# Two graph-attention layers on one core: two more nested Strassen products per matrix, added up inside one PSUM bank, and the order of every engine taken from a list schedule in the source

## The chip, the cores and the metric

The kernel runs on one core of one Trainium2 chip. The metric is the device time of one execution in microseconds (us); lower is better. A core has five instruction queues that matter here: PE (TensorE, the matrix array; its weight loads are shown apart as PEld), DVE (VectorE), ACT (ScalarE), POOL (GpSimd) and SP (SyncE, which here only issues DMAs). Each engine works through its own queue strictly in order. All arithmetic is in 32-bit floats.

## The reference

There are 128 independent graphs of 128 nodes with 512 features, and two attention layers of 8 heads, the second on the output of the first:

```python
# layer 0
Q, K, V = (x @ W + b for W, b in ...)            # 8 heads of 64
scores  = Q K^T / 8 + a_i + c_j + b_g + log(adj + 1e-9)    # a = x @ w_g[:D], c = x @ w_g[D:]
x       = softmax(scores) @ V + x
# layer 1
q, k, v = (x @ W.T + b for W, b in ...)
logits  = q k^T / 8 + log(max(adj, 1e-8))
out     = (softmax(logits) @ v) @ Wo.T + bo
x       = layer_norm(x + out) * gamma + beta
```

## The kernel before, in words

**Tiling.** Four graphs are one group, so that a projection is a 512 x 512 by 512 x 512 product. `t` counts 64 steps: `t` below `NG` = 32 is layer 0 of group `t`, the rest is layer 1 of group `t - NG`. A step has the matrices v, q and k, and in layer 1 the output projection o of the group before it. That makes 223 matrices in all; the o of the very last group is done graph by graph with plain matmuls. The exponentials of the scores are multiplied by the adjacency (`weigh`), which takes the place of adding its logarithm. Layer 0 writes its result to DRAM (`x1d`), and layer 1 reads it again.

**Strassen twice.** Every matrix is computed by Winograd's form of Strassen's scheme: seven products P1 to P7 of 256 x 256 blocks instead of eight (`Strassen`). The sums of weight blocks are made once (`combine_outer`), the sums T1 to T4 of input blocks once for each step, by POOL (`sums`). A plain product (`product`, L280) is 8 matmul instructions that stream 256 columns; one instruction fills one half of the output partitions, and the two halves run side by side in the array. Inside some of the seven products the same scheme is used again (`inner`, L339): seven products of 128 x 128 blocks, that is 14 matmul instructions that stream 128 columns. In the text these are **wide** and **narrow** matmuls. `INSIDE` (L174) says where: in P2 and P4 of nearly all matrices, in P2 alone or nowhere at the start of each layer. The inner products run in four phases. After each phase DVE adds pieces of the PSUM bank onto a copy in SBUF (`onto`, `add`), and the outer additions are done in the same instructions.

**Biases and rows.** The q and k biases are added by ACT while it copies from PSUM (`copy`). The v bias of layer 0 and the o bias of layer 1 are added to the natural-layout input tile `xn` by POOL (`add_row`, L267); `onto_x` and `residual` (L548), both on POOL, then add `xn` to the result.

**Attention.** `scores` (L444) takes all four graphs of a group in one go: 32 matmuls that use half the array's rows each (64 x 128 tiles, shown as 64\*128), where every projection matmul uses half of its columns (128 x 64 tiles, shown as 128\*64). Two double-sized PSUM buffers, and two banks borrowed from the projections for the third graph, hold them. ACT takes the exponential, DVE multiplies by the adjacency, `mix` forms attention times v for two graphs at a time, and DVE normalises.

**Order.** Each instruction is kept where the program has it (`InOrder`, every instruction is recorded on L132, so that all lines of the profile say L132 and the tiles' names tell them apart). The order is written by hand: a row of slots, seven to a matrix (`SLOTS`, L55), says which product comes when, and `put(pre/post, slot, ...)` hangs every load, sum, addition and store on a slot. Tiles come from pools with two to four buffers; the sums T1 to T4 have two each.

Of the kernel before, what the change touches and what calls it, by code (L numbers as in the profile page):

```python
# [41 lines left out]
class Strassen:  # L42

    A11, A12, S4, NA22, S1, S2, S3 = range(7)

    SLOTS = (("P1", "P4.1 b"), ("P4 b",), ("P3 b", "P4.2 b"), ("P6", "P4.3 b"), ("P5", "P4.4 b"), ("P7",), ())  # L55
# [5 lines left out]
    PHASES = {"1": ("P1", "P2", "P5"), "2": ("P6",), "3": ("P7",), "4": ("P4", "P3")}  # L61


    RAW = {(0, 0): A11, (1, 0): A12, (1, 1): NA22, (0, 1): S3}

# [25 lines left out]
    @staticmethod  # L91
    def combine_inner(v, t, x, ks=slice(0, 2)):

        q, x = t[:, Strassen.A12 : Strassen.NA22 + 1 : 2][:, ks], x[:, ks]
        low, high = slice(0, P), slice(P, 2 * P)
        Strassen.combine(
            v, q[:, :, 0, low], q[:, :, 1, low], q[:, :, 0, high], q[:, :, 1, high], x[:, :, 0], x[:, :, 1], x[:, :, 2]
        )

    @staticmethod  # L100
    def inner_weight(t, x, i):

        k = i == "P4"
        q, low, high = t[:, Strassen.NA22 if k else Strassen.A12], slice(0, P), slice(P, 2 * P)
        return {
            "P1": q[:, 0, low], "P2": q[:, 1, low], "P3": x[:, k, 2], "P4": q[:, 1, high],
            "P5": x[:, k, 0], "P6": x[:, k, 1], "P7": q[:, 0, high],
        }


class InOrder:


    ENGINES = ("tensor", "vector", "scalar", "gpsimd", "sync")

    def __init__(self, tc):
        self.nc = tc.nc
        for name in self.ENGINES:
            setattr(self, name, InOrder.Engine(tc, getattr(tc.nc, name)))

    def __getattr__(self, name):
        return getattr(self.nc, name)

    class Engine:
        def __init__(self, tc, engine):
            self.tc, self.engine = tc, engine

        def __getattr__(self, name):
            f = getattr(self.engine, name)
            if not callable(f):  # L130
                return f
            return lambda *args, **kw: self.tc.keep_in_program_order(f(*args, **kw))  # L132


def fast_path(ctx, tc, args, GOOD, bad):
# [5 lines left out]

# [3 lines left out]
    nc = InOrder(tc)  # L149
# [6 lines left out]
    SCALE = 1.0 / HD**0.5  # L156
    HALVES = slice(0, P // 2), slice(P // 2, P)
    assert N == P and HD == 64 and KC == 4 and G == 4 and NG * G == B

    const = ctx.enter_context(tc.tile_pool(name="const", bufs=1))  # L160
    weights = ctx.enter_context(tc.tile_pool(name="weights", bufs=4))
    act = ctx.enter_context(tc.tile_pool(name="act", bufs=1))
    work = ctx.enter_context(tc.tile_pool(name="work", bufs=2))
    small = ctx.enter_context(tc.tile_pool(name="small", bufs=2))
# [3 lines left out]
    XTB = [act.tile([P, G, KC, N], F32, name=f"xT_{i}") for i in range(2)]  # L168
    X1D = [dram.tile([G, N, D], F32, name=f"x1d_{g}") for g in range(NG)]
    LAST = 2 * NG  # L170
    XN, XT, TS, AD, QT, KT, V, C, GATE, RC, OR, AT, TO, HS, MV, RS = ({} for _ in range(16))
    WQ, WK, WV, WO, BQ, BK, ROWS = ({} for _ in range(7))

    INSIDE = {t: ("P2", "P4") if t and t != NG else ("P2",) if t else () for t in range(LAST)}  # L174
    INSIDE.update({("qk", NG): (), ("o", NG): ()})
    INSIDE.update({("o", t): ("P2", "P4") if t > NG else () for t in range(NG, LAST)})

# [3 lines left out]

    def load_tiles(t):
        XT[t] = XTB[t % 2]
        AD[t] = act.tile([P, G, N], F32, tag="adjT", name=f"adjT_{t}", bufs=2)

    def load_graph(t, b, engine):

        L, g = split(t)
        src = x[g * G : (g + 1) * G] if L == 0 else X1D[g]
        xs = src.rearrange("b (t i) (c q f) -> q i b c t f", i=S, q=Q, f=S)  # L190
        for q in range(Q):
            rows = slice(q * S, (q + 1) * S)
            engine.dma_start(XT[t][rows, b].rearrange("i c (t f) -> i c t f", f=S), xs[q, :, b])

    def load_adjacency(t, engine):
        _, g = split(t)
        adjs = adj[g * G : (g + 1) * G].rearrange("b (t i) (q f) -> q i (b t) f", i=S, f=S)
        for q in range(Q):
            rows = slice(q * S, (q + 1) * S)
            engine.dma_start(AD[t][rows].rearrange("i b (t f) -> i (b t) f", f=S), adjs[q])  # L200

    def load(t):
        load_tiles(t)
        for b in range(G):
            load_graph(t, b, nc.sync)

    def load_natural(t, *engines):
        L, g = split(t)
        src = x[g * G : (g + 1) * G] if L == 0 else X1D[g]
        for k in range(2):  # L210
            XN[t, k] = act.tile([P, 2, D], F32, tag="xn", name=f"xn_{t}_{k}", bufs=4)
# [22 lines left out]
    def sums(Bs, name, s):  # L234
        a, b = Strassen.SUMS[s]
        Bs[s] = act.tile([P, 2, 2, N], F32, tag=s, name=f"{s}_{name}", bufs=2)
        nc.gpsimd.tensor_tensor(Bs[s], Bs[a], Bs[b], ALU.subtract)

    def inner_sums(Bs, name, i="P2"):

        q = Bs[Strassen.OPERANDS[i][1]]
        y = act.tile([P, 4 if i == "P2" else 3, N], F32, tag=f"inner{i}", name=f"inner{i}_{name}", bufs=2)
        b11, b12, b21, b22 = q[:, 0, 0], q[:, 1, 0], q[:, 0, 1], q[:, 1, 1]
        t1, t2, t4 = (y[:, i] for i in range(3))
        t3 = y[:, 3] if i == "P2" else b12
        nc.gpsimd.tensor_tensor(t1, b12, b11, ALU.subtract)
        nc.gpsimd.tensor_tensor(t2, b22, t1, ALU.subtract)
        nc.gpsimd.tensor_tensor(t3, b22, b12, ALU.subtract)
        nc.gpsimd.tensor_tensor(t4, t2, b21, ALU.subtract)
        Bs[i, "inner"] = {"P1": b11, "P2": b21, "P3": b22, "P4": t4, "P5": t1, "P6": t2, "P7": t3}  # L250


    def gate(t, b, s):

        if (b, s) == (0, 0):
            C[t] = small.tile([P, 2, G], F32, tag="c", name=f"c_{t}", bufs=2)
        nc.gpsimd.tensor_tensor(GW[:, 2 + s], XN[t, b // 2][:, b % 2], GW[:, s], ALU.mult)

    def gate_sum(t, b, s):
        o = GW[:, 2 + s]  # L260
        nc.scalar.activation(o, o, AF.Identity, accum_out=C[t][:, s, b : b + 1])

    def gate_exp(t):
        GATE[t] = small.tile([P, G], F32, tag="gate", name=f"gate_{t}", bufs=2)
        nc.scalar.activation(GATE[t], C[t][:, 0], AF.Exp, bias=bg)

    def add_row(t, k):  # L267


        for b in (1, 0):  # L270
            xn = XN[t, k][:, b]
            nc.gpsimd.tensor_tensor(xn, xn, ROWS[split(t)[0]], ALU.add)


# [5 lines left out]
    def product(i, W, Bs, bank, side, first):  # L280
# [5 lines left out]
        for o in range(2):  # L286
            for k in range(2):
# [5 lines left out]
                matmul(dst, lhsT, rhs, first and o == 0 and k == 0, k == 1)  # L293
# [5 lines left out]
    def matrix(n, name, W, Bs, side, out_tile, dst, bias=None, inside=("P2",)):  # L299

        t = {}
        C12, C21 = block(0, 1, side), block(1, 0, side)

        def bank(tag):
            return ps.tile([P, 4 * N], F32, tag=tag, name=f"{tag}{name}")

        def biased(m):
            return [(slice(2 * k * N, 2 * (k + 1) * N), bias()[:, 2 * m + k : 2 * m + k + 1]) for k in range(2)]  # L310

        def copy(o, i, m):

            if bias is None or m is None:
                if len(o.shape) == 3:
                    i = i.rearrange("p (h d) -> p h d", d=o.shape[2])
                nc.scalar.copy(o, i)
            else:
                for h, b in biased(m):
                    nc.scalar.activation(o[:, h], i[:, h], AF.Identity, bias=b)  # L320

        def kept(tag, i, m, bufs):
            t[tag] = work.tile([P, 4 * N], F32, tag=tag, name=f"{tag}{name}", bufs=bufs)
            copy(t[tag], i, m)

        def add(m, n, i, v, lo=0, hi=4, shift=0):


            for lo, hi, o in dst(m, n, lo, hi):
                p, s = i[:, (lo + shift) * N : (hi + shift) * N], v[:, lo * N : hi * N]  # L330
                if len(o.shape) == 3:
                    p, s = (r.rearrange("p (h d) -> p h d", d=o.shape[2]) for r in (p, s))
                nc.vector.tensor_tensor(o, p, s, ALU.add)

        def onto(v, b, i, at):
            v = v[:, b * N : (b + 1) * N]
            nc.vector.tensor_tensor(v, i[:, at * N : (at + 1) * N], v, ALU.add)

        def inner(i, phase):  # L339

            m, v = (1, t["u3"]) if i == "P4" else (0, t["t1"])
            if phase == "1":
                t[i] = bank("p1") if i == "P2" else t["a"]
            p, a, b = t[i], Strassen.inner_weight(*t["W"], i), t["B"][i, "inner"]
            for k, j in enumerate(Strassen.PHASES[phase]):
                at = {"P2": 0, "P5": C12, "P3": C12}.get(j, C21)
# [740 lines left out]
```

## Time and profile before

| what | us |
|---|---|
| three runs | 3147.54, 3147.86, 3148.11; median 3147.86 |
| profiled execution, first to last instruction | 3146.3 |
| PE busy | 3130.7 |
| POOL busy | 2344.3 |
| DVE busy | 2104.3 |
| ACT busy | 985.2 |

The profiled execution lies 1.6 us under the median of the runs. One step of layer 0 takes 42.7 us and one of layer 1 54.6 us, by the starts of neighbouring score groups in the timeline (1033.58 and 1076.31; 2500.03 and 2554.58). The span is practically one row of matmuls: the first product starts at 8.06 us, the last matmul ends at 3133.9 us, and 12.4 us of layer norm and stores follow. The DMA queue of SP issues 2,578 transfers, about 0.65 us apart when they follow one another.

### The profile page before, as it was taken

To read this page: it belongs to the slowest core of one execution; us is meant where nothing else is said; L and a number is where in the kernel's file an instruction comes from. 1 tells how busy PE (TensorE), PEld (TensorE's weight loads), DVE (VectorE), ACT (ScalarE), POOL (GpSimd) and SP (SyncE) were. 2 spreads that over 40 slices of the span, in tenths; PEclk is the share of its full clock that TensorE was granted. 3 is DMA by queue.
4 is the path that set the end of the run, shared out by engine and by line. 5 is a ranking of instruction groups with operands and counts; after the bars stand their busy time and mean duration, and the time that the engine had idled before them with its cause. 6 is when DMAs were issued, how large, how long until landed. Compare 5 with 4: busy or idle time off the path is not lost.

```text
span 3146.3 us, 102048 instructions
## 1 busy us (share of the span) xinstructions
PE 3130.7 (100%) x42570; PEld 2510.6 (80%) x42570; DVE 2104.3 (67%) x4941; ACT 985.2 (31%) x1927; POOL 2344.3 (75%) x2732
## 2 busy tenths in 40 slices
PE   9999999999999999999999999999999999999998
PEld 7777777777777777777888888788888888787885
DVE  6666666666666666666676667667666766667666
ACT  3333333333333333332222222222222222222222
POOL 8776767676766676786877878787877878787876
PEclk9999999999999999999999999999999999999999
DMA  5333333333333333442434334343434334343432
GB/s 136 81 82 86 85 83 80 74 82 85 86 82 85 69 88 81 101 112 54 100 70 89 82 74 93 76 97 73 96 75 82 89 74 94 75 99 72 95 68 80
DMA packets 1017279, 266.28 MB, mean 85 GB/s; under 512 B 942704, under 2 KB 949872, under 8 KB 1016816
## 3 DMA queue, kind: packets, MB, share of 16 engines
q1 hardware_dynamic: 1015152, 257.34, 37.2%
q8 instruction: 340, 5.57, 0.7%
q10 hardware_dynamic: 1408, 2.10, 0.2%
q14 instruction: 123, 1.01, 0.1%
q0 software_dynamic: 256, 0.26, 0.0%
HBM read 159.92 MB, written 67.11 MB: 72 GB/s over the span
## 4 chain that ended last, share of the span: by engine, by line
PE 99%; DVE 0%; DMA 0%; ACT 0%; issue 0%; ACTq 0%; DVEq 0%
PE p3v L132 10%; PE p0q L132 10%; PE p3k L132 10%; PE av L132 8%; PE p2k L132 7%; PE p2v L132 7%; PE p2q L132 7%; PE p0o L132 7%; PE s L132 6%; PE p0v L132 4%; PE p3q L132 4%; PE p0k L132 4%; PE p2o L132 3%; PE p1k L132 3%; PE p1q L132 3%; PE p1v L132 3%
## 5 line engine op out<-in xcount | busy, mean ns | idle before, releaser
L132 POOL TENSOR_TENSOR gw<-xn,gw 128x512 f32<-128x512 f32 x256 | 323.7, 1281 | 103.6 <-ACT gw L132 100.8
L132 POOL TENSOR_TENSOR xn<-xn,row 128x512 f32<-128x512 f32 x256 | 328.0, 1304 | 2.0 <-DMA bq<-in_L_gnn_bq_dram 2.0
L132 POOL TENSOR_TENSOR T<-xT 128x512 f32<-128x512 f32 x128 | 193.6, 1512 | 138.4 <-DVE xT L132 133.7
L132 POOL TENSOR_TENSOR xn<-o,xn 128x512 f32<-128x512 f32 x128 | 161.0, 1281 | 147.1 <-DVE o L132 147.1
L132 POOL TENSOR_TENSOR h<-h,xn 128x512 f32<-128x512 f32 x124 | 161.2, 1322 | 115.8 <-DVE h L132 115.7
L132 PE MATMUL p3k<-T,wk 128*64 128x256 f32 (+1 forms) x2068 | 234.3, 350 | 0.0
L132 PE MATMUL p3v<-wv,T 128*64 128x256 f32 (+1 forms) x2068 | 225.9, 351 | 0.0
L132 PE MATMUL p0q<-T,wq 128*64 128x256 f32 (+1 forms) x2068 | 225.0, 350 | 0.0
L132 PE MATMUL s<-qT,kT 64*128 64x128 f32 x3088 | 200.4, 276 | 0.2 <-DVE xT L132 0.2
L132 PE MATMUL av<-v,e 128*64 128x65 f32 x6272 | 199.6, 221 | 0.0
L132 PEld LDWEIGHTS av<-v,e 128*64 128x64 f32 x6272 | 196.5, 137 | 0.1
L132 DVE TENSOR_TENSOR e<-e,adjT 128x1024 f32<-128x1024 f32 x98 | 150.7, 1538 | 65.5 <-ACT e L132 65.5
L132 PEld LDWEIGHTS s<-qT,kT 64*128 64x128 f32 x3088 | 182.7, 188 | 11.7 <-issue 11.4
L132 PEld LDWEIGHTS p3k<-T,wk 128*64 128x64 f32 x2068 | 154.1, 137 | 46.5
L132 PEld LDWEIGHTS p3v<-wv,T 128*64 128x64 f32 x2068 | 141.4, 137 | 56.4
L132 PEld LDWEIGHTS p0q<-T,wq 128*64 128x64 f32 x2068 | 142.0, 137 | 54.3
L132 POOL TENSOR_TENSOR h<-h,gamma 128x512 f32<-128x512 f32 x121 | 154.7, 1278 | 27.9 <-ACT h L132 27.9
L132 DVE STREAM_TRANSPOSE xT<-xT 128x512 f32<-128x512 f32 x252 | 173.4, 697 | 0.5 <-DMA xT<-in_x_dram 0.5
L132 ACT ACTIVATE gw<-gw 128x512 f32<-128x512 f32 x256 | 160.9, 630 | 39.1 <-POOL gw L132 39.1
L132 POOL TENSOR_TENSOR h<-h,beta 128x512 f32<-128x512 f32 x121 | 154.9, 1280 | 9.5
L132 PE MATMUL p0o<-wo,T_o 128*64 128x256 f32 (+1 forms) x1368 | 155.6, 353 | 0.5 <-ACT u3o L132 0.5
L132 PEld LDWEIGHTS p0o<-wo,T_o 128*64 128x64 f32 x1368 | 106.7, 137 | 30.1 <-ACT u3o L132 0.8
(315 smaller groups left out, 8088.6 us busy)
## 6 DMA issues: line engine op xcount, KB each, us to landing
x1d<-xn SPq DMA_DIRECT2D x64, 512.0 KB, 3.0
xT<-x1d SPq DMA_DIRECT2D x512, 64.0 KB, 2.5
xn<-x1d SPq DMA_DIRECT2D x64, 512.0 KB, 6.3
xT<-in_x_dram SPq DMA_DIRECT2D x496, 64.0 KB, 2.8
xn<-in_x_dram SPq DMA_DIRECT2D x62, 512.0 KB, 4.5
aT<-o SPq DMA_DIRECT2D x984, 32.0 KB, 1.9
out_dram<-h SPq DMA_DIRECT2D x60, 512.0 KB, 4.5
adjT<-in_adj_dram SPq DMA_DIRECT2D x256, 64.0 KB, 3.7
```

Of the source, the lines that this page charges most:

```text
L132: return lambda *args, **kw: self.tc.keep_in_program_order(f(*args, **kw))
```

## The change

The whole of the fast path is written anew; what is computed stays the same.

1. **Two more nested products.** P1 and P5 also use the inner scheme, in every matrix but six (v, q and k of the first step of each layer, which have none). The program then has 12,152 narrow and 5,544 wide matmul instructions, where it had 6,062 and 9,024.
2. **The inner product is added up within its bank.** ACT first writes zeros into two blocks of the bank. Narrow matmuls accumulate onto what lies there, and between phases ACT copies one block to another and one to SBUF (`s5`), and DVE adds twice within the bank. The outer additions follow on whole banks.
3. **Other work moves.** The v and o biases are added by DVE as it copies from PSUM (`row=ROW`), so that `add_row` is gone. The residual of layer 1 is an accumulating DMA issued from POOL in place of a POOL addition. `root` and `shift` use DVE in part.
4. **Attention one graph at a time.** `scores` has one PSUM buffer of two banks, `mix` one bank and works by half graphs, each at a place of its own. The buffers of the projections are the banks A0, A1, B, C and D. Tiles are placed once; T1 to T4 have a single buffer each.
5. **The order.** `Plan` records every operation with the tiles it touches and a cost from a formula, and `schedule` runs a list scheduler forwards and backwards twelve times over the whole program. Instructions are issued in order of the best start times. A vector operation that waits for a DMA therefore stands in DVE's queue where the formula has the data landed.

In the program order that results, all 256 score groups of 8 matmuls stand alone; before there are 63 of 32 and two of 16.

```diff
-    SLOTS = (("P1", "P4.1 b"), ("P4 b",), ("P3 b", "P4.2 b"), ("P6", "P4.3 b"), ("P5", "P4.4 b"), ("P7",), ())
-    PHASES = {"1": ("P1", "P2", "P5"), "2": ("P6",), "3": ("P7",), "4": ("P4", "P3")}
+    INSIDE = ("P1", "P2", "P4", "P5")
...
+class Plan:
+    HOP, DRAIN, MARGIN = 0.1, 0.17, 0.25
+    PATIENCE, PASSES = 40.0, 12
...
+    def cost(engine, method, aps, accumulates):
...
+        if method == "dma_start":
...
+            return 0.6, 2.2 + kb / 150
+        if engine == "scalar":
+            return (0.15 + 0.00086 * n + 0.2 * accumulates,)
+        if engine == "vector":
+            if method in ("transpose", "bn_stats"):
+                return (0.01 + 0.00133 * n,)
+            return (0.15 + (0.00106 if psum or len(aps) < 3 else 0.00135) * n,)
+        return (0.2 + 0.00215 * n,)
...
+    def wait(self, p, o):
+        if p.engine == o.engine and not p.lag:
+            return 0.0
+        return p.lag + self.HOP + self.DRAIN * (p.engine == "tensor") + self.MARGIN * (o.engine == "tensor")
...
-        def inner(i, phase):
-            m, v = (1, t["u3"]) if i == "P4" else (0, t["t1"])
...
-                matmul(p[:, at * N : (at + 1) * N], x, y, phase == "1" and k == 0, True)
-            if phase == "1":
-                onto(v, 0, p, C21)
-                add(m, 0, p, v, 0, 1)
...
+    def inner(i, W, Bs, bank, side, pos):
...
+        nc.scalar.copy(blocks[:, C21 : 4 : 3 - C21], ZERO)
+        leaves(pos[0], ("P5", 3), ("P1", C21))
+        nc.scalar.copy(s5, blocks[:, 3])
+        nc.scalar.copy(blocks[:, 0], blocks[:, C21])
+        leaves(pos[1], ("P2", 0), ("P6", C21))
+        nc.vector.tensor_tensor(blocks[:, C12], blocks[:, C21], s5, ALU.add)
+        leaves(pos[2], ("P3", C12), ("P7", C21))
+        nc.vector.tensor_tensor(blocks[:, 3], blocks[:, C21], s5, ALU.add)
+        leaves(pos[3], ("P4", C21))
...
+        make("P1", a, True)
+        copy(t1, a, 0)
+        make("P6", a, False)
+        copy(u2, a, 0)
+        make("P2", c, True)
+        add(0, 0, c, t1)
+        make("P7", a, False)
+        copy(u3, a, 1)
+        make("P5", b, True)
+        add(1, 1, b, u3)
+        make("P3", b, False)
+        add(0, 1, b, u2)
+        make("P4", d, True)
+        add(1, 0, d, u3)
...
-    def scores(t, graphs, spare=None):
...
+    def scores(t, b, e, pos):
+        k, s = b // 2, SCORES
+        with nc.unit(pos, 0.92):
+            for c in range(KC):
+                for r in range(2):
...
+                    nc.tensor.matmul(s[:, r, c], KT[k][at], QT[k][at], start=True, stop=True)
+        s = s.rearrange("p r c j -> p (r c) j")
+        nc.scalar.activation(s, s, AF.Exp, scale=SCALE, **({"bias": C[t][:, 1, b : b + 1]} if t < NG else {}))
+        nc.vector.tensor_tensor(e, s, AD[t][:, b : b + 1].to_broadcast([P, H, N]), ALU.mult)
...
-    def residual(t, n):
-        for b in range(2):
-            h = HS[t, n][:, b]
-            nc.gpsimd.tensor_tensor(h, h, XN[t, n][:, b], ALU.add)
+    def residual(t, k):
+        nc.gpsimd.dma_start(HSB[k], X1D[split(t)[1]][2 * k : 2 * k + 2].rearrange("b p d -> p b d"), accum_op=ALU.add)
...
-    for i in range(-1, max(max(pre), max(post), 7 * len(mats) + 3) + 1):
-        for u in pre.get(i, []):
-            u()
...
+    nc.issue()
```

## The prediction, made before the changed kernel had run

> **What bounds the kernel now.** I read the page first, then PE's waits, then the timeline of a stretch of layer 0. TensorE is busy for the whole span at full granted clock:
>
> ```profile
> span 3146.3 us, 102048 instructions
> PE 3130.7 (100%) x42570; PEld 2510.6 (80%) x42570; DVE 2104.3 (67%) x4941; ACT 985.2 (31%) x1927; POOL 2344.3 (75%) x2732
> PEclk9999999999999999999999999999999999999999
> ```
>
> In the table of PE's waits six waits add up to 3.1 us, so nobody holds it up:
>
> ```profile
> engine line waited for: us in total, times, longest us
> PE p0v L132 <- DVE wv L132: 0.9, 1, 0.9
> PE p0o L132 <- ACT u3o L132: 0.5, 1, 0.5
> ```
>
> So the time is the sum of the matmuls' own pace, and the pace is read from starts in the timeline (durations include the pipeline's latency; one matmul shows as two records):
>
> ```profile
> 1020.28 1.90 PE L132 MATMUL p2k<-T,wk 128*64 128x256 f32 x16
> 1022.01 0.39 PE L132 MATMUL p0q<-innerP,wq 128*64 128x128 f32 x4
> 1022.23 0.39 PE L132 MATMUL p0q<-T,wq0i 128*64 128x128 f32 x4
> 1022.44 0.39 PE L132 MATMUL p1k<-innerP,wk0i 128*64 128x128 f32 x4
> 1022.66 1.90 PE L132 MATMUL p3k<-T,wk 128*64 128x256 f32 x16
> 1024.39 0.39 PE L132 MATMUL p1k<-innerP,wk 128*64 128x128 f32 x4
> ```
>
> A plain product takes 1.73 us (1020.28 to 1022.01); three block products take 0.65 us (1022.01 to 1022.66), 0.217 us each, with no gap between different banks or sizes.
>
> **The change, part by part.**
>
> *Matmuls removed.* A nested product is 7 x 0.217 = 1.52 us in place of 1.73, 0.21 us less. Narrow matmuls go from 6,062 to 12,152; at 14 to a product that is 435 products more, so 435 x 0.205 (between 1.73 and 1.72, as other products start) = **-89 us**.
>
> On narrow matmuls a rule speaks against the change: the Trainium skill's page "TensorEngine Tiling (Array Packing)", section Performance Considerations, Instruction Overhead, charges each matmul some 60 cycles, and there are 2,610 more of them; at the 2.4 GHz of "TensorE: Matmul & The Clock Gate" my estimate from the pages would be 65 us lost. The rows above show none: eight wide matmuls take 1.73 us and sixteen narrow ones would take 8 x 0.217 = 1.74.
>
> *Scores alone.* The same timeline shows what a group of scores costs beside its own work, since it uses another shape of tile:
>
> ```profile
> 1033.26 0.39 PE L132 MATMUL p3k<-T,wk0i 128*64 128x128 f32 x4
> 1033.58 2.06 PE L132 MATMUL s<-qT,kT 64*128 64x128 f32 x32
> 1035.47 1.06 PE L132 MATMUL s_p<-qT,kT 64*128 64x128 f32 x16
> 1036.36 1.06 PE L132 MATMUL s<-qT,kT 64*128 64x128 f32 x16
> 1037.35 1.95 PE L132 MATMUL p0v<-wv,T 128*64 128x256 f32 x16
> 1039.13 0.61 PE L132 MATMUL p1v<-wv,xT 128*64 128x128 f32 x8
> ```
>
> The last narrow matmuls would be through at 1033.26 + 0.22 = 1033.48, and the scores begin 0.10 later. One graph in the middle takes 0.89 (1035.47 to 1036.36); the four take 3.77, which is 0.21 more than 4 x 0.89. The product behind them takes 1.78, 0.05 more. So each change to the other shape and back costs 0.36 us, which I take as 0.35 for rounding. The new order has 256 such changes where there were 65: 191 x 0.35 = **+67 us**. The planner's cost of a score group, 0.92, holds only the 0.89. Half graphs of `mix` have the projections' own tile shape and cost nothing: in the timeline a narrow product starts at 1005.85 and `mix` behind it at 1006.07, 0.22 later.
>
> The tensor queue alone thus gives 3147.9 - 89 + 67 = 3126. This is made on the profiled 3146.3 and carried to the median, 1.6 above.
>
> *ACT, DVE, POOL.* Their instructions in the new program by rows of the old:
>
> ```profile
> L132 DVE TENSOR_TENSOR u3k<-p3k,u3k 128x128 f32<-128x128 f32 x141 | 41.1, 292 | 107.6 <-PE p3k L132 104.7
> L132 DVE TENSOR_TENSOR v<-p2v,u3v 128x512 f32<-128x512 f32 x64 | 43.6, 681 | 0.0
> L132 ACT COPY u3v<-p3v 128x512 f32<-128x512 f32 x47 | 27.6, 587 | 203.1 <-PE p3v L132 203.0
> L132 ACT ACTIVATE t1q<-p0q,bq 128x256 f32<-128x256 f32 x94 | 39.5, 471 | 51.7 <-PE p0q L132 51.7
> ```
>
> DVE gets 1,736 block additions (x 0.29 = 503) and 1,081 additions or row copies of 512 columns (x 0.68 = 735); with 252 multiplications by the adjacency at 1.21, 440 transposes at 0.69 and the small operations of normalising I come to some 2,430 us, 78% of the span. ACT gets 868 zero fills and 1,736 block copies, some 770 us by the line through 0.587 at 512 columns and 1.027 at 1,024, and comes to 1,780. POOL loses 256 row additions (328 us in its table) and 124 residual additions (161) and comes to some 2,100. No row shows ACT or DVE adding into a bank; the nearest, ACT's exponential in place in PSUM, costs what the one into SBUF does (1,027 against 1,025 ns), so I take no surcharge; a tenth more would be some 80 us on queues with over 600 us to spare. None becomes the bound as a sum. The cost is in **waits**, since PE depends on round trips PE-DVE-PE and PE-ACT-PE within each nested product, and PE's covers are short:
>
> (a) Round trips by themselves. I laid the new order's matmuls end to end at the paces above and compared every pause of a PSUM tile with the work between at row durations plus 0.26 us for two hand-overs (ACT and DVE start some 0.21 after the last matmul is issued). In 32 of 4,055 pauses the work is longer, by 12 us together: **+12**. This assumes that DVE and ACT are free; at 78% DVE often isn't, but the planner leaves 0.25 on each wait of PE. Low end 0. High end: 0.1 us for each of 868 nested products, 87.
>
> (b) Transfers that DVE waits for. The source lets a 64 KB load land 0.6 + 2.63 = 3.2 us after its issue and puts the transpose there or behind. Rows say:
>
> ```profile
> xT<-in_x_dram SPq DMA_DIRECT2D x496, 64.0 KB, 2.8
> adjT<-in_adj_dram SPq DMA_DIRECT2D x256, 64.0 KB, 3.7
> xn<-x1d SPq DMA_DIRECT2D x64, 512.0 KB, 6.3
> ```
>
> x fits. The adjacency is 0.5 us late at the median, and up to 7.6 - 3.2 = 4.4. While DVE waits for it, the block additions behind it in its queue wait, and PE behind those. 64 steps x 0.5 = 32, less what PE has in hand and what DVE still has to do: in the new order 14 DVE operations, some 5.3 us by rows, stand between the last use of the old adjacency and the transpose of the new. I take **+20**. Low 0, if DVE is busy elsewhere when it lands; high 64 x 1.5 = 96 (SP issues twenty loads in a row 0.05 us slower each than the source has it, 1 us).
>
> (c) The residual's accumulating DMA, 31 times two. No row shows one. Bounds: 3.0 (the 512 KB store to `x1d`) and 12.6 (the 512 KB load at 6.3, paid twice, for it also reads what it adds to). The source allows 0.6 + 5.6; between the two last writes and the first statistics DVE has only 2.4 to 6.6 us of other work. Nearest row: the load, 6.3, on an emptier queue. I take **0**; the high end is (12.6 - 6.4) x 31 = 190. "DMA: Bandwidth & Descriptors", Anatomy of one DMA, fits 2.0 us plus bytes at 436 GB/s for a DMA from POOL; 3.2 us here, an estimate from the page by which it would never be late.
>
> (d) Single buffers for T1 to T4: from the last matmul on the old T4 to the first on the new one lie some 4.1 us of matmuls; POOL needs 1.28 + 0.73. Start and tail: a few us either way. **0**.
>
> Sum: 3126 + 12 + 20 = **3158 us**, 0.3% slower: the saved matmuls are given back by the change of tile shape, and short waits, which were absent before, decide the sign. A measurement of this kernel can tell 0.2%, 6 us, from no change.
>
> **The rivals.**
>
> *Faster: the waits stay hidden* (31%). The score groups make PE 4 x 0.35 = 1.4 us a step slower than planned, and this is slack for everybody else; then (b) is 0 and the time is 3126 + 12 = 3138. For it: the planned margins, and idle DVE time. Against it: a queue in order at 78% in which one late load stops four nested products.
>
> *Much faster: the change of shape is free where it meets a wait anyway* (6%): 3147.9 - 89 + 12 = 3071. Against it: all 65 old changes cost the same, groups of two graphs and of four.
>
> *Slower still: the accumulating DMA holds DVE* (11%). Place: the first statistics of each layer-1 step; price 31 us for each us after 6.4; with a landing at 8.4 it is 62 us, 3220.
>
> *Slower still: DVE's queue makes PE wait in every product* (12%): 868 x 0.1 = 87 in place of the 12, 3233. For it: DVE at 78%; against it: 0.25 us margins.
>
> **How the numbers follow.** The forecast has 40%, with 3140 to 3190 as its own range. Faster by over 0.2% (below 3142): the 6, 24 of the 31 and 4 of the 40, 34%. Within: 7 and 9, 16%. Slower: 27 of the 40 and the two last rivals, 50%. The range 3116 to 3230 leaves out the 6% below and about half of the two slow rivals.
>
> **What would show it.** Nested products at 0.217 a block and narrow records doubled, with wide ones down to three fifths (the first term). Scores standing alone, with 0.1 before them and 0.25 within and behind (second). PE's table of waits: DVE and ACT, with tens of us in total, and in the waits of DVE adjacency and `h` transfers (third). I am wrong if PE's waits stay under 15 us, if the score changes cost less than 0.2, or if PE idles over 100 us.

## The result, and the profile after

The changed kernel takes **3389.6 us** (median of four runs, 3384.41 to 3391.71), the kernel before 3148.0: 1.0765 times as long, 95% interval 1.075 to 1.0781. Its profiled execution spans 3387.9 us, against 3146.3. The page of the changed kernel, with busy time, granted TensorE clock and the shares of the chain of waits:

```profile
span 3387.9 us, 115982 instructions
...
PE 3191.8 (94%) x47790; PEld 2657.8 (78%) x47790; DVE 2240.5 (66%) x5287; ACT 1612.3 (48%) x4396; POOL 2063.8 (61%) x2245
...
PEclk9999999999999999999999999999999999999999
...
PE 68%; SPq 14%; DMA 6%; issue 4%; POOL 4%; DVE 3%; ACT 0%; DVEq 0%; POOLq 0%; ACTq 0%
```

DVE, ACT and POOL are all further from full than forecast. PE is idle for 196 us, where the prediction had named 100 as a sign of being wrong, and the chain runs for 14% of the span through SP's queue, which computes nothing.

**Where the time went, by steps.** From the starts of neighbouring score groups in the timeline (mean of 27 steps in the middle of each layer):

| kernel | layer-0 step | layer-1 step | total |
|---|---|---|---|
| before | 42.7 | 54.6 | 3148.0 |
| changed | 42.7 | 62.2 | 3389.6 |

Layer 0 lost nothing. By the same starts, 4.2 us are lost before the first scores of layer 1 (at 1420.7 instead of 1416.5; the first step alone takes 47.6), 22.6 in the first three steps of layer 1 (178.6 for 156.0), 208.7 in its other 28 (1737.9 for 1529.2) and 6.1 behind the start of the last step's scores: 241.6 us, the whole difference.

**Layer 0 is the tensor queue that was forecast.** PE's timeline there (start, duration, two records to a matmul):

```profile
310.90 0.39 PE L298 MATMUL bankB<-wi,innerT 128*64 128x128 f32 x4
311.12 0.39 PE L298 MATMUL bankB<-w,T 128*64 128x128 f32 x4
311.44 1.16 PE L298 MATMUL s<-qT,kT 64*128 64x128 f32 x16
312.53 0.44 PE L298 MATMUL bankC<-wi,innerB 128*64 128x128 f32 x4
312.80 0.39 PE L298 MATMUL bankC<-w,xT 128*64 128x128 f32 x4
```

A block takes 0.22 (310.90 to 311.12). The scores start 0.10 after the last block is through (311.12 + 0.22), the next block 0.20 after 0.89 of scores, and that block takes 0.05 more: 0.35 us for a visit of the other tile shape.

**In layer 1 DVE waits for transfers.** The largest of PE's waits is now for DVE's additions within bank B, 95.2 us; before, all of PE's together were 3.1. From the table of DVE's waits (for what, us in total, times, longest):

```profile
DVE gw L298 <- DMA gw<-o: 138.3, 37, 5.6
...
DVE xT L298 <- DMA xT<-x1d: 72.4, 60, 3.1
...
DVE adjT L298 <- DMA adjT<-in_adj_dram: 36.3, 22, 3.1
...
DVE st L298 <- DMA h<-x1d: 24.9, 20, 2.6
```

PE waits for DVE, and DVE waits for the moved attention output (`gw`), 37 times in 31 steps and up to 5.6 us, then for `x`, and for the adjacency less than for either; `st`, the statistics of the layer norm, wait for the accumulating DMA. All of DVE's waits for transfers come to 291 us. One such place, first in SP's queue, then DVE's, then PE's (the bracket is the idle time before and what ended it):

```profile
2430.98 10.98 SPq L298 DMA_DIRECT2D gw<-o  x16
2442.06 1.92 SPq L298 DMA_DIRECT2D xT<-x1d  x3
2444.08 11.34 SPq L298 DMA_DIRECT2D gw<-o  x16
```
```profile
2458.02 1.31 DVE L298 STREAM_TRANSPOSE gw<-gw 128x512 f32<-128x512 f32 x2 [4.76 <-DMA gw<-o]
2459.25 0.27 DVE L298 TENSOR_TENSOR bankB<-bankB,s 128x128 f32<-128x128 f32 x1
```
```profile
2455.93 0.39 PE L298 MATMUL bankD<-innerT,wi 128*64 128x128 f32 x4
2459.57 0.44 PE L298 MATMUL bankB<-T,wi 128*64 128x128 f32 x4 [3.26 <-DVE bankB L298]
```

SP issues 35 transfers from 2430.98 to 2455.42, that is 24.4 us, 0.70 us each. The schedule charges 0.6, or 21.0 us, and puts the transposes where the data would have landed by that. They are 3.4 us late before the landing is even counted; DVE stands for 4.76 us, three additions into banks behind the transposes stand with it, and PE has work for part of that time and then stops for 3.26 us. A landing itself is nearly on time at the median: for 32 KB the formula allows 0.6 + 2.4 = 3.0 us, for 512 KB 6.2. Of the 992 moves 233 take longer than their 3.0, up to 8.0; what late landings cost is the question of run 2.

```profile
gw<-o SPq DMA_DIRECT2D x992, 32.0 KB, 2.0
h<-x1d POOLq DMA_DIRECT2D x62, 512.0 KB, 6.4
```

### The profile page after: what moved, and what is told of

The parts are those of the page before. It is cut to its first block, busy times and chain, and to the rows that moved or that the text cites. A ratio compares the mean times of both kernels' runs of the same rounds, so it can differ in the third digit from the quotient of the medians.

```text
span 3387.9 us, 115982 instructions
## 1 busy us (share of the span) xinstructions
PE 3191.8 (94%) x47790; PEld 2657.8 (78%) x47790; DVE 2240.5 (66%) x5287; ACT 1612.3 (48%) x4396; POOL 2063.8 (61%) x2245
## 4 chain that ended last, share of the span: by engine, by line
PE 68%; SPq 14%; DMA 6%; issue 4%; POOL 4%; DVE 3%; ACT 0%; DVEq 0%; POOLq 0%; ACTq 0%
PE bankA L298 24%; PE bankB L298 16%; SPq L298 14%; PE bankC L298 8%; PE bankD L298 7%; PE s L298 7%; PE av L298 6%; DMA h<-x1d 2%; DMA gw<-o 2%; DMA adjT<-in_adj_dram 1%; POOL T L298 1%; DMA xT<-x1d 1%; POOL xn L298 1%; POOL innerB L298 1%; DVE gw L298 1%
## 5 line engine op out<-in xcount | busy, mean ns | idle before, releaser
L298 PE MATMUL bankA<-T,w 128*64 128x256 f32 x4096 | 521.0, 381 | 3.7 <-ACT t L298 3.7
L298 PEld LDWEIGHTS bankA<-T,w 128*64 128x64 f32 x4096 | 274.7, 137 | 93.9 <-ACT t L298 4.9
L298 PE MATMUL bankA<-w,T 128*64 128x256 f32 x2048 | 265.2, 382 | 2.6 <-DVE u L298 2.6
L298 PE MATMUL bankB<-xT,w 128*64 128x256 f32 x2048 | 254.5, 382 | 8.2 <-DVE qT L298 5.1
L298 DVE TENSOR_TENSOR bankB<-bankB,s 128x128 f32<-128x128 f32 x434 | 127.3, 293 | 166.9 <-PE bankB L298 140.8
L298 ACT ACTIVATE s<-s 128x1024 f32<-128x1024 f32 x128 | 128.9, 1007 | 143.9 <-PE s L298 138.8
L298 PEld LDWEIGHTS bankB<-xT,w 128*64 128x64 f32 x2048 | 141.9, 138 | 62.8 <-DVE qT L298 10.0
L298 ACT ACTIVATE s<-s,c 128x1024 f32<-128x1024 f32 x128 | 139.3, 1088 | 91.2 <-PE s L298 90.9
L298 DVE STREAM_TRANSPOSE gw<-gw 128x512 f32<-128x512 f32 x124 | 83.9, 695 | 144.6 <-DMA gw<-o 138.3
L298 DVE TENSOR_TENSOR h<-s,adjT 128x1024 f32<-128x1024 f32 x128 | 155.7, 1216 | 33.2 <-ACT s L298 33.2
L298 POOL TENSOR_TENSOR gw<-w,gw 128x512 f32<-128x512 f32 x128 | 164.0, 1298 | 19.7 <-ACT gw L298 18.9
```

Of the source, the lines that this page charges most:

```text
L298: self.tc.keep_in_program_order(getattr(getattr(self.nc, engine), method)(*args, **kw))
```

## The experiments

Three causes were set against each other. The **pace**: 0.70 us an issue on SP against the schedule's 0.6 adds up over bursts of 35, and DVE's queue passes the lateness on. The **round trips** between PE, DVE and ACT within the nested products. The **landing**: each transfer, above all the accumulating DMA, lands later than the schedule has it. Each expectation says itself what its letters stand for; the text uses these names.

### 1 to 3: the schedule's cost of a transfer

Only the formula changes, and with it the order that the list schedule chooses:

```diff
-            return 0.6, 2.2 + kb / 150
+            return 0.7, 2.2 + kb / 150      # run 1: pace
+            return 0.6, 3.7 + kb / 150      # run 2: landing
+            return 0.7, 3.7 + kb / 150      # run 3: both
```

> Only the planner's cost of issuing a transfer goes from 0.6 to 0.7 us (the trace of the changed kernel has SP issue 54 transfers in 38 us of one layer-1 step, 0.70 each). Theory A, DVE's queue stands before transposes whose transfers the order expects too early because SP issues more slowly than the planner has it: the layer-1 step (now some 62 us) falls to 56 to 59 us and the time to 3200 to 3290 us. Rival B, the tile-shape changes of the scores, which the planner has too cheap, make the layer-1 loss: within 30 us of the 3389.6. Rival C, the accumulating DMA of the residual: within 30 us. Layer-0 steps stay at 42.6 on average for all.

> Only the planner's time from issue to landing grows by 1.5 us (2.2 to 3.7 plus size), issue stays at 0.6. Theory A, if it is the landing and not the pace: 3200 to 3290 us. If it is SP's pace in bursts, a lag of 1.5 us still covers the lateness of the first twenty transfers of a burst, so part of it: 3250 to 3350. Rivals B and C: B within 30 us of 3389.6; C, where the accumulate's landing is what is late, falls as far as A.

> Both planner constants, 0.7 to issue and 1.5 us more to land. Theory A: DVE's waits for transfers (285 us in the changed kernel) go under 60, the layer-1 step to 54 to 56 us, the time to 3130 to 3190. Rival B: within 30 us of 3389.6. A fourth, D, that DVE at 66 to 78% is simply too full to serve round trips in order: DVE's waits for transfers vanish but PE's waits stay, 3300 or more.

| run | total | ratio to before | layer-1 step | DVE's wait for `gw` / `xT<-x1d` / `st` |
|---|---|---|---|---|
| changed | 3389.6 | 1.0765 | 62.2 | 138 / 72 / 25 |
| 1 pace | 3245.0 | 1.0309 (1.028 to 1.0339) | 57.2 | 27 / 71 / 26 |
| 2 landing | 3366.0 | 1.0694 (1.0663 to 1.0725) | 61.5 | 96 / 112 / 0 |
| 3 both | 3248.3 | 1.032 (1.029 to 1.035) | 57.4 | 12 / 36 / 0 |

A tenth of a microsecond an issue is worth 145 us. 1.5 us for a landing is worth 24, although it takes the wait for the accumulating DMA away altogether; so the landing falls as the main cause. Run 2 came out 16 us above what it expected for a late pace (3250 to 3350). With both, DVE's waits for transfers fall to 80 us, from 171 in run 1, and the time is no better than with the pace alone. The third run missed its expectation (waits under 60, total 3130 to 3190), which left open whether the pace is the whole cause or round trips hold the last 3.4 us over the 54.0 of the tensor queue (54.6 - 8 x 0.205 + 3 x 0.35).

### 4: twice the visits of the scores

Each score group is cut into two units, a quarter of a position apart; the scheduler separates most of them (429 visits where there were 256).

```diff
-        with nc.unit(pos, 0.92):
-            for c in range(KC):
+        for part in range(2):
+            with nc.unit(pos + 0.25 * part, 0.46):
+                for c in (2 * part, 2 * part + 1):
```

> Each score group of 8 matmuls is split into two of 4 at two places of the order: 429 visits of the other tile shape in place of 256. If a visit costs 0.35 us as read from the trace of before, PE loses 173 x 0.35 = 60 us: 3450, and the spacing above nominal at score boundaries goes from some 76 us to some 135. If visits are cheap where PE is free of waits, within 20 us of 3389.6. The order shifts elsewhere too, so the layer-0 steps, which have no waits, are the ones to read: 42.6 should become 43.5.

3405.7 us: the total missed the expected 3450 and by itself would fit cheap visits. Layer 0, where nothing else waits, has 222 visits in place of 128, in its middle 7 a step in place of 4, and its step grows by 0.95 to 1.05 us, by the 27 steps that are taken (42.7 to 43.6 or 43.7): 0.32 to 0.35 us a visit, against 0.35 read off the timeline. The price of the tile shape is shown there. Layer 1 doesn't show it (61.8 after 62.2); that its pauses for other reasons cover it is likely but not shown.

### 5: the same order, fewer transfers

Every engine keeps the order of the changed kernel, and twelve of SP's 54 transfers in each step of layer 1 are struck out after scheduling. The output is then made from old adjacencies and partly old attention outputs.

```diff
+                nc.left_out = q == i                  # in move
                 nc.sync.dma_start(d[q * S : (q + 1) * S, :, i], src)
+            nc.left_out = t > NG
             load_adjacency(t)
+            if o.i in self.out:                       # in issue
+                continue
```

> The order of all engines is the changed kernel's, instruction for instruction, but of the 54 transfers that SP issues in a step of layer 1 twelve are left out where the program is written (the four adjacency loads and the 4 + 4 moves of attention output whose two quarters have the same number), so the output is not the reference's. All matmuls, additions, copies and transposes stay. Theory A (SP issues at 0.70 us what the schedule has at 0.6, and everything planned around a landing slips): 42 x 0.70 = 29.4 us is less than the 54 x 0.6 = 32.4 that the schedule reckons with, so the slip is gone: layer-1 step 55 to 57.5 us in place of 62, total 3185 to 3255. Theory B (round trips between PE, DVE and ACT within the nested products are what is late): nothing of these is changed, 3360 to 3390. Theory C (transfers land late, not issue late): lateness of the others stays, at most a fifth of the gain, 3330 to 3390.

**3196.6 us**, ratio 1.0153 (1.0136 to 1.017): 193 of the 242 us are gone, with no matmul, addition or copy moved. The same burst in this kernel's SP queue:

```profile
2330.19 9.83 SPq L303 DMA_DIRECT2D gw<-o  x12
2340.12 1.93 SPq L303 DMA_DIRECT2D xT<-x1d  x3
2342.15 9.12 SPq L303 DMA_DIRECT2D gw<-o  x12
```

It ends 21.1 us after it began, which is what the schedule reckons with for 35 issues (21.0). The 27 transfers come 0.78 us apart here, slower than 0.70, so that the burst is shortened by less than the count promised. DVE's waits:

```profile
DVE gw L303 <- DMA gw<-o: 9.9, 13, 2.1
```

The wait for `gw` falls from 138.3 to 9.9, although 24 of its 32 moves remain. SP's queue, which is behind its place in the schedule, is shown to be the bulk of the loss; round trips by themselves would have left all of it, and a late landing of the transfers that remain most of it. The adjacency's landing went with the struck loads, but DVE's waits for it were 36.3 us of 291.

### 6 to 8: what the last 3.4 us of a layer-1 step are

Runs 6 and 7 start from run 3 (3248.3; step 57.4), run 8 reckons with like costs. From run 8 on the scheduler also makes 20 passes in place of 12, in runs 8 and 10 with its constant `PATIENCE` at 25 in place of 40.

```diff
# run 6
-            nc.sync.dma_start(AD[t][rows].rearrange("i b (t f) -> i (b t) f", f=S), adjs[q])
+            (nc.scalar if t > NG else nc.sync).dma_start(AD[t][rows].rearrange("i b (t f) -> i (b t) f", f=S), adjs[q])
# run 7
-    INSIDE = ("P1", "P2", "P4", "P5")
+    INSIDE = ("P4", "P5")
# run 8 (0.8 us an issue, 3.7 a landing, 0.2 a hand-over, 0.2 margin)
-                nc.sync.dma_start(d[q * S : (q + 1) * S, :, i], src)
+                (nc.scalar if (q == i or q + i == 1) else nc.sync).dma_start(d[q * S : (q + 1) * S, :, i], src)
```

> As the run with 0.7 us an issue and 3.7 us a landing in the schedule's costs (3248), with the four adjacency loads of each layer-1 step issued from ACT's queue in place of SP's (50 issues left on SP). Theory A: SP's 54 issues are still what a layer-1 step is arranged around; with 4 x 0.70 = 2.8 us less on SP the step falls by 1 to 2.5 us from 57.3, total 3175 to 3225. Theory B (round trips of the nested products hold the rest): unchanged, 3240 to 3255, or more, since ACT issues in addition.

> As the run with 0.7 us an issue and 3.7 us a landing (3248), but only P4 and P5 nested, P1 and P2 plain: some 434 nested products fewer. In layer 0 the step must grow by 6 x 0.205 = 1.2 us to 43.8 in either theory. In layer 1 the tensor queue alone would grow by 8 x 0.205 = 1.6 us. Theory A (layer 1 is arranged around SP, TensorE has idle time): the layer-1 step stays within 1 us of 57.3 and the total is 3270 to 3300. Theory B (each nested product costs PE a wait, 0.1 us or more): the layer-1 step falls by over 1 us below 57.3, total 3220 to 3260. If TensorE were the only bound: step 58.9, total 3330.

> The changed kernel with six of the sixteen moves of each pair of graphs issued from ACT's queue (42 issues a step left on SP) and a schedule that reckons with 0.8 us an issue, 3.7 us a landing, 0.2 us a hand-over and 0.2 us of margin. Theory A: with SP no longer short the layer-1 step comes within 2 us of its tensor queue's 54.0: total 3140 to 3190. Theory B (round trips of the nested products): layer-1 step stays at 57, total 3235 to 3260.

| run | total | ratio to before | layer-0 step | layer-1 step |
|---|---|---|---|---|
| 6 adjacency from ACT | 3205.8 | 1.0188 (1.0171 to 1.0205) | 42.6 | 55.9 |
| 7 two products nested | 3234.5 | 1.0272 (1.0255 to 1.0289) | 43.8 | 55.8 |
| 8 six moves from ACT | 3201.0 | 1.0171 (1.0154 to 1.0188) | 42.5 | 56.1 |

Run 6 takes 2.8 us of issuing off SP and the step falls by 1.5, as the pace would have it. Run 8 stays 11 us above what the pace expected; its step is still 2.1 us over the 54.0 of the tensor queue. Run 7 speaks for the round trips: with half the nested products a layer-1 step is 1.6 us *shorter*, although its matmuls alone take 1.6 us longer. It is then close to its floor (54.0 + 8 x 0.205 = 55.6). DVE also has less to do there (2062.6 us busy against 2237.7 in run 3), and the run can't tell a shorter DVE queue from fewer round trips. In layer 0 the same edit costs 1.2 us a step, which is 6 x 0.205 and confirms the price of nesting.

### 9 to 11: towards a version that beats both

Four products nested in layer 0, three in layer 1, two of sixteen moves on ACT's queue, and costs raised in the formula:

```diff
-    HOP, DRAIN, MARGIN = 0.1, 0.17, 0.25
+    HOP, DRAIN, MARGIN = 0.2, 0.17, 0.1                # run 10: 0.1, 0.17, 0.2
-            return 0.6, 2.2 + kb / 150
+            return 0.75, 3.7 + kb / 150                # run 10: 0.8, 2.6
+    SOME = ("P2", "P4", "P5")                          # layer 1; run 10: P1, P4, P5
-        with nc.unit(pos, 0.92):
+        with nc.unit(pos, 1.25):                       # run 10: 0.92
```

In runs 9 and 10 the product that is plain in layer 1 multiplies by a weight that was already combined for nesting, so that their output isn't the reference's while the work is the same; run 11 is run 9 without that combination.

> Towards a version that beats both: layer 0 with all four products nested, layer 1 with P2, P4 and P5 (P1 plain), two of the sixteen moves of each pair on ACT's queue, and a schedule that reckons with 0.75 us an issue, 3.7 us a landing, 1.25 us a score group, 0.2 us a hand-over and 0.1 us of margin. The tensor queue alone: layer-0 step 42.6; layer-1 step 54.0 + 4 x 0.205 = 54.8. Theory A (SP's issues were the cause, and what is left in layer 1 is time that the schedule itself leaves TensorE idle around them): layer-1 step 54.8 to 55.6, total 3150 to 3185. Theory B (every nested product costs a wait in layer 1): layer-1 step about 56.5, half-way between the 55.7 with two nested products and the 57.3 with four, total 3200 to 3215. Faster than before (under 3142) by neither.

> As its neighbour, but P1, P4 and P5 nested in layer 1, and 0.8 us an issue, 2.6 us a landing, 0.92 us a score group, 0.1 us a hand-over and 0.2 us of margin. Theory A: layer-1 step 54.8 to 55.8, total 3150 to 3190. Theory B: layer-1 step about 56.5, total 3200 to 3215.

> The first of the two runs with three nested products in layer 1 (3162.9), with the weights of layer 1 combined inside only for the three products that are nested there (P1's are left as they are, which its plain product needs). Four groups of small POOL operations fewer at the start of layer 1; nothing else changes. Theory A: 3160 to 3164, layer-1 step 54.7, its tensor queue. Slower than before (3148) by 12 to 16 us, as the tensor queue has 0.1 us a layer-1 step more than before's 54.6 and the first step and the step into layer 1 are some 5 us longer each.

3162.9, 3168.5 and 3162.9 us; layer-1 steps 54.7, 54.9 and 54.7. Run 11 against before: 1.0046 (1.0029 to 1.0063). From its page:

```profile
span 3161.2 us, 112680 instructions
...
PE 3135.0 (99%) x46302; PEld 2565.6 (81%) x46302; DVE 2192.5 (69%) x5039; ACT 1508.0 (48%) x4024; POOL 2050.4 (65%) x2225
```

PE is full again, DVE's wait for `gw` is down to 1.3 us, and three nested products in layer 1 run at the matmuls' own pace (54.0 + 4 x 0.205 = 54.8). So the round trips need not cost anything either: a schedule with higher costs and three nested products hides them. Which of the changes made together in these runs does it was not tried. No version beats before: where nothing waits, the visits of the scores have taken back what the nested products save (layer-0 step 42.6 against 42.7, layer-1 step 54.7 against 54.6). The 14.9 us that run 11 takes longer lie before the first scores of layer 1 (5.8, the first step above all), in layer 1 (3.2) and behind the start of the last step's scores (5.9). Whether some schedule brings four nested products in layer 1 to their 54.0 stays open; the best tried have 55.9.

## Why the prediction was right and wrong, point by point

- **Matmuls removed, -89 us: right.** Nesting two products more shortens a layer-0 step by 1.2 us for six products, 0.2 each (run 7 against run 3), and no charge for the doubled number of narrow instructions appears.
- **Scores alone, +67 us: right.** 0.35 us read off the timeline after the change, 0.32 to 0.35 by run 4. The Trainium skill's page "TensorEngine Tiling (Array Packing)", Key Properties, says that changing the tiling mode drains TensorE; the trace agrees, with pauses of 0.10 us before the scores and 0.20 behind them.
- **The tensor queue as a whole: right where it is the bound.** By these two terms layer 0 should come out at 42.7 - 1.2 + 1.05 = 42.5; it is 42.7.
- **Sums of the engines:** too high, DVE 2,430 against 2240.5, ACT 1,780 against 1612.3, POOL 2,100 against 2063.8. Right in what mattered: none is a bound.
- **(a) Round trips, +12: right in layer 0.** PE's table of waits has 0.6 us there between 50 and 1416 us. In layer 1 round trips can't be told from what starts them: four nested products leave 3.4 us a step over the tensor queue (run 3) and three leave none (run 11), under another schedule.
- **(b) Transfers that DVE waits for, +20, high end 96: the step that failed.** The mechanism was the right one (a load late, DVE stopped in order, PE behind it), but I priced the landing of a single adjacency load, 0.5 us late, and took SP's pace for no more than "twenty loads in a row 0.05 us slower each than the source has it, 1 us". In the changed kernel that load lands after 2.6 us at the median, within the 3.2 allowed. The transfers that mattered were the moves of attention output, which that step didn't name, in bursts of 35 with 0.10 us too much on each: 3.4 us at the end of each burst, and 7.5 us a step over before by the time that PE has paid for `gw`, `x`, the adjacency and the slow clock behind its stops. The 0.05 holds for most issues, which start 0.65 apart, and is half of the 3.4; the other half is a few issues in each burst that take 1.1 us and more (last section), which the step left out. 193 of the 242 us lie here by run 5, which holds the order fixed. The row was in the trace of before, in SP's own timeline:

```profile
2515.89 22.45 SPq L132 DMA_DIRECT2D aT<-o  x32
```

32 moves in 22.45 us are 0.70 each. Set against 0.6 in the source, a step with 54 issues is 5.4 us behind, times 31 steps 167 us: an estimate of the term that the sum lacked, outside every case that I gave a chance, and still below the 193 that run 5 gives back.
- **(c) Accumulating DMA, 0: right in the main.** It landed after 6.4 us at the median where the schedule allows 6.2, and DVE waited 24.9 us for it. Run 2 takes this wait away and gains 24 us by all that it changes; run 3 takes it away too and is no faster than run 1, which has it. As the rival with 62 us it falls with that.
- **(d) Start and tail, 0: wrong by 10 us.** 4.2 and 6.1 us, and run 11 has nearly the same (5.8 and 5.9), so they hardly come from SP's pace. What they come from was not tried. The 22.6 us of the steps into layer 1 do not remain there (155.0 for 156.0).
- **The rival of DVE's queue** (PE waits in every product) was right that DVE holds PE, but had neither the price (3233) nor the place: 59 waits of PE of over 1 us, about two a step and up to 4.5 us long, make up 139 of its 176 us in layer 1.

## What to carry to other kernels

A static schedule is as good as the cost that it has most too low: read the pace of every queue, the DMA-issuing ones too, from a burst in the trace and set it against the schedule's number, times the length of the burst. A late transfer is paid by the consumer's whole queue, so look for the operation that an in-order engine reaches before its data, not for the engine's busy share. Then test it by striking out transfers with the order held fixed; that separates a late queue from everything that a new order changes besides.

## What the runs showed of the hardware

The clock falls after a pause. Behind the pause of 3.26 us shown above, the windows of the same stretch (us; PE busy, PEld, DVE, ACT, POOL with instruction counts; PE clock granted; DMA share; GB/s):

```profile
2460.00:2464.00 4.00, 4.00 (x46) 3.74 (x42) 2.48 (x6) 0.81 (x3) 3.92 (x5) 0.57 0.60 95
2464.00:2470.00 6.00, 6.00 (x88) 5.22 (x86) 5.06 (x11) 2.69 (x7) 5.84 (x9) 1.00 0.96 249
```

From 0.7 us after it, for 3.4 us, the blocks start 0.43 apart instead of 0.22; the clock in the first row is a mean, 0.57, of full and half. The record of the granted clock has 26 such stretches at half clock in layer 1, 22 of 3.41 us and four of twice that, most of them behind a stop of PE of 2.3 to 4.5 us. By the matmuls that start in them they cost some 46 us, 1.2 to 1.8 us in each 3.41. The mean clock was 0.983, and 0.999 in run 11, where PE's waits add up to 20 us. The Trainium skill's page "TensorE: Matmul & The Clock Gate", in "What's actually happening", gives a window of about 3.4 us, after an idle one of which the clock is half. The trace agrees with that length; the stop shown above, 3.26 us, was shorter than a whole window.

The issue of a transfer has no fixed price. These are single moves from the bursts of the changed kernel (the first two) and of run 5:

```profile
2438.21 0.61 SPq L298 DMA_DIRECT2D gw<-o  x1
2438.87 1.14 SPq L298 DMA_DIRECT2D gw<-o  x1
2338.24 1.78 SPq L303 DMA_DIRECT2D gw<-o  x1
```

Half of all moves take up to 0.61 us and start 0.65 apart. Of the 992 moves of the changed kernel 114 take over 0.9 us, 1.36 on average, and of the 744 of run 5 92, 1.39. Three of these among 27 issues make the 0.78 there, two among 35 and a pause of 0.3 us the 0.70 here. What makes an issue long is open. The Trainium skill's page "DMA: Bandwidth & Descriptors", Rules for kernel authors, says that spreading DMAs over several engines' queues doesn't raise bandwidth and only saves issue time. Here issue time was the thing in short supply, and four loads a step on ACT's queue were worth 43 us (run 6).
